# Norms on VectorE in the last half blocks, a residual by identity products, and unread products before the last turns

## The chip, the cores and the metric

The kernel runs on one core of one Trainium2 chip. A core has a matrix engine (TensorE, PE in the profile; its weight loads are PEld), three engines for elementwise work (VectorE or DVE, ScalarE or ACT, GpSimd or POOL), and a queue that issues transfers (SyncE or SP). Each takes its own instructions in order; they wait for each other by semaphores. The metric is the time of one execution on the device in microseconds (us), lower is better.

## The reference

One graph attention layer, over 8 frames of 2048 nodes with 256 channels, inside an outer residual and norm. The adjacency mask is one for all frames. Cut to what matters:

```python
q, k, v = split(x @ w_qkv)                       # 8 heads of 32 channels
scores = einsum('fnhd,fmhd->fhnm', q, k) / sqrt(32)
attn = softmax(where(adj > 0, scores, -1e9))
t = einsum('fhnm,fmhd->fnhd', attn, v)
y = layernorm(x + t) * g1 + be1
f = relu(y @ w1 + b1) @ w2 + b2
z = layernorm(y + f) * g2 + be2
out = layernorm(x + z)                           # no gain, no offset
```

Each row of the output passes through three norms. The last sum, `x + z`, is called the third residual here.

## The kernel before, in words

**Items.** `fast_path` walks over *items* `(f, qc, g, mb)`: frame, block of 512 query rows, group of four heads, and block of 128 key rows, `mb` from 0 to 15. For each item PE makes scores with keys on the partitions (L276), DVE adds the mask on the way from PSUM to SBUF in two halves of 128x1024 (L279), ACT exponentiates 128x2048 in place (L283), PE multiplies by the values (L310). The softmax sums are made from the exponentiated tiles: POOL adds some of them (L339), accumulating transfers add others (L336), and PE reduces the four tiles that remain (L382, "denominators").

**Order.** Each engine's order is that of the program text. Scores run two items ahead of the values. All other work (the `fill` list) consists of generators that `advance` resumes once per item: `yield 1` lets one item go by, `yield BANK` asks for a PSUM bank, and PE work draws on a *credit* per item, so a generator without credit waits for the next item unless it is due. While the loop runs only one bank is free for this side work (`bank()`, with `state["side"]` set), so a new product in that bank has to wait until the old one has been read.

**Rows.** When a query block is finished, `outcome` turns the attention output back to rows on PE and divides (`divide`, L427), adds `x`, and starts `tail`: norm (`norm`: statistics on DVE at L348 and L349, the factors `rs` and `nb` on POOL at L353 to L357, the application on ACT at L360), the two feed-forward products (`feed_forward`, L575 to L601), a second norm, `g2` and `be2` on POOL (L441, L443), the residual `x`, a third norm, and the store (L449). Normally the residual comes by an accumulating transfer; for the last block but one (block 2 of the last frame) DVE adds `xb`, a copy of `x` loaded earlier, at L411.

**The last block.** Its second head group (`ENDING`) is cut differently: 16 items of two key blocks by 256 query rows, half 0 first and then half 1 (scores L264, masks L268, values L298, output copy L303, POOL additions L330). Each half's rows are finished by a generator `closing(h)`: denominators (L490, five tiles), their sum (L493), turned sums and reciprocal (L504), turned output and division (L522), plus `x` (L525), statistics (`half_stats`, L456 and L457, `rs` on POOL at L459 and L460), first norm (`half_norm`: `nb` on DVE at L465, application on ACT at L467), POOL's row copy with `g1` and `be1 + b2` (L531, L532), turned rows and their scaling on ACT (L537), w1 (L545 copies it out), w2, the sum (L555), second norm, `g2` and `xb` on DVE (L560, L561), third norm, store (L565). Counts of the sums for a final range check (L508, L509, L971 to L982) go along.

After the loop `advance` is called until the list is empty. PE products through the helper `columns` have line L54, turns through `transposes` line L95.

Of the kernel before, what the change touches and what calls it, by code (L numbers as in the profile page):

```python
# [10 lines left out]
F32 = mybir.dt.float32  # L11
# [4 lines left out]
AF = mybir.ActivationFunctionType  # L16
ALU = mybir.AluOpType
AX = mybir.AxisListType

P = 128  # L20
# [41 lines left out]
def fast_path(ctx, tc, cst, x, adj, out, RS):  # L62
    nc = tc.nc
# [24 lines left out]
    def columns(out, lhsT, rhs, start, stop):  # L88
        state["credit"] -= 4 * out.shape[-1]
        in_columns(nc, out, lhsT, rhs, start, stop)  # L90
# [310 lines left out]
    def outcome(f, qc):  # L401
        yield ROOM
        state["tails"] += 1
        xin = x[f, qc * CH:(qc + 1) * CH, :].rearrange("(p j) c -> p j c", p=P)
        y = yp.tile([P, TPC, C], F32, name="y")
        begin = items.index((f, qc, 1, LAST)) + SUM + 2
        yield from divide(f, qc, y)
        if (f, qc) == (F - 1, NCK - 2):
            yield 1
            xb = state["xb"]  # L410
            nc.vector.tensor_tensor(y, y, xb, ALU.add)  # L411
            start(begin + 3, tail(f, qc, y, xin, 2, xb), begin + 18)
            return
        nc.gpsimd.dma_start(y, xin, accum_op=ALU.add)
        if (f, qc) == (F - 1, NCK - 3):
            start(begin + 10, tail(f, qc, y, xin, 2), begin + 18)
        else:
            start(begin + 10, tail(f, qc, y, xin), begin + 26)
# [12 lines left out]
    def tail(f, qc, y, xin, per=1, xb=None):  # L431
        yield from norm(y, per)
        yield from feed_forward(y)
        if xb is not None:
            nc.gpsimd.tensor_tensor(xb, xb, rows(cst["be2r"]), ALU.add)
        yield 1
        z = y
        yield from norm(z, per if per == 1 else TPC)
        while xb is None and per > 1 and state["now"] % MB not in CALM:
            yield 1  # L440
        nc.gpsimd.tensor_tensor(z, z, rows(cst["g2r"]), ALU.mult)  # L441
        yield 1
        nc.gpsimd.tensor_tensor(z, z, rows(cst["be2r"]) if xb is None else xb, ALU.add)  # L443
        yield 1
        if xb is None:
            nc.gpsimd.dma_start(z, xin, accum_op=ALU.add)
            yield 7 if per == 1 else 10
        yield from norm(z, per)
        nc.sync.dma_start(out[f, qc * CH:(qc + 1) * CH, :].rearrange("(p j) c -> p j c", p=P), z)  # L449
        state["tails"] -= 1  # L450

    def half_stats(t):
        mv = small.tile([P, 2, nc.vector.BN_AGGR_DIM], F32, name="mv")
        for j in range(2):
            st = small.tile([P, nc.vector.BN_STATS_DIM], F32, name="st")
            nc.vector.bn_stats(st, t[:, j, :])  # L456
            nc.vector.bn_aggr(mv[:, j, :], st)  # L457
        rs = small.tile([P, 2], F32, name="rs")
        nc.gpsimd.tensor_scalar(rs, mv[:, :, 1], EPS, 1.0, op0=ALU.add, op1=ALU.mult)  # L459
        nc.gpsimd.tensor_tensor(rs, rs, cst["mhalf"][:, 0:2], ALU.pow)  # L460
        return mv, rs

    def half_norm(t, mv, rs):
        nb = small.tile([P, 2], F32, name="nb")
        nc.vector.scalar_tensor_tensor(nb, mv[:, :, 0], -1.0, rs, op0=ALU.mult, op1=ALU.mult)  # L465
        for j in range(2):
            nc.scalar.activation(t[:, j, :], t[:, j, :], AF.Identity, bias=nb[:, j:j + 1], scale=rs[:, j:j + 1])  # L467

    def closing(h):
        f, qc, g = ENDING  # L470
        own, part, t0 = slice(2 * h, 2 * h + 2), slice(h * HQ, (h + 1) * HQ), len(items) - MB // 2 * (2 - h)
        terms = [(5, 6), (1, 7), (0, 7), (6, 8), (7, 8)]
        dst = out[f, qc * CH + h * HQ:qc * CH + (h + 1) * HQ, :].rearrange("(p j) c -> p j c", p=P)

        def row2(v):
            return v[:, None, :].to_broadcast([P, 2, C])

        yield BANK
        ps = bank()
        for n, (block, when) in enumerate(terms):  # L480
            if n:
                yield MORE
            while state["now"] < t0 + when:
                yield WAIT
            term = PT.pop((*ENDING, block + h * MB // 2))
            state["credit"] -= 4 * CH
            for b in range(2):
                for i in range(4):
                    r = D * i
                    nc.tensor.matmul(ps[r:r + D, 0:HQ], cst["halves"][:, g, :], term[:, i, b * HQ:(b + 1) * HQ],  # L490
                                     start=(n + b == 0), stop=(n + b == len(terms)))
        dT = DT[f, qc]
        nc.vector.tensor_tensor(dT[:, part], ps[:, 0:HQ], dT[:, part], ALU.add)  # L493
        if h == 0:
            state["y"] = yp.tile([P, TPC, C], F32, name="y")
            state["ff"] = [work.tile([P, 2, CH], F32, name=n) for n in ("turned", "hT")]
        y, (yT, hT) = state["y"][:, own], state["ff"]
        xr, xb = (t[:, own] for t in state["rows"])
        def turned_sums():
            ps = bank()  # L500
            transposes(ps, [dT[:, part][:, j::2] for j in range(2)])
            den = ps[:, 0:HQ].rearrange("p (j c) -> p j c", c=P)[:, :, ::D // 2]
            rc = op.tile([P, 2, H], F32, name="rc")
            nc.vector.reciprocal(rc, den)  # L504
            return rc, den

        def count(den):
            nc.vector.tensor_tensor(RS[:, 0, own], RS[:, 0, own], den, ALU.add)  # L508
            nc.vector.tensor_tensor(RS[:, 1, own], RS[:, 1, own], den, ALU.min)  # L509

        yield 1
        if h == 0:
            yield BANK
            rc, den = turned_sums()
            count(den)
        yield BANK
        po = bank()
        transposes(po, [OT[f, qc, gg][:, part][:, j::2] for gg in range(2) for j in range(2)])
        if h:
            rc, den = turned_sums()  # L520
        for gg in range(2):
            nc.vector.tensor_tensor(y[:, :, gg * P:(gg + 1) * P].rearrange("p j (h d) -> p j h d", d=D),  # L522
                                    po[:, gg * HQ:(gg + 1) * HQ].rearrange("p (j h d) -> p j h d", h=4, d=D),
                                    rc[:, :, gg::2, None].to_broadcast([P, 2, 4, D]), ALU.mult)
        nc.vector.tensor_tensor(y, y, xr, ALU.add)  # L525
        found = half_stats(y)
        if h:
            count(den)
        yield 1
        half_norm(y, *found)  # L530
        nc.gpsimd.tensor_tensor(xr, y, row2(cst["g1r"]), ALU.mult)  # L531
        nc.gpsimd.tensor_tensor(xr, xr, row2(cst["be1b2r"]), ALU.add)  # L532
        yield BANK
        ps = bank()
        transposes(ps, [y[:, j, a * P:(a + 1) * P] for a in range(2) for j in range(2)])
        for a in range(2):
            nc.scalar.activation(yT[:, a, part], ps[:, a * HQ:(a + 1) * HQ], AF.Identity,  # L537
                                 bias=cst["be1c"][:, a:a + 1], scale=cst["g1c"][:, a:a + 1])
        yield 1
        for d in range(2):  # L540
            yield BANK
            ps = bank()
            for a in range(2):
                columns(ps[:, 0:HQ], w1s[:, a, d * P:(d + 1) * P], yT[:, a, part], start=(a == 0), stop=(a == 1))
            nc.scalar.activation(hT[:, d, part], ps[:, 0:HQ], AF.Relu, bias=cst["b1s"][:, d:d + 1], scale=1.0)  # L545
        yield 1
        yield BANK
        ps = bank()
        for j in range(2):
            if j:  # L550
                yield MORE
            for d in range(2):
                columns(ps[:, j * C:(j + 1) * C], hT[:, d, part][:, j * P:(j + 1) * P], w2s[:, d, :], start=(d == 0), stop=(d == 1))
        z = y
        nc.vector.tensor_tensor(z, ps.rearrange("p (b c) -> p b c", c=C), xr, ALU.add)  # L555
        found = half_stats(z)
        yield 1
        half_norm(z, *found)
        yield 1
        nc.vector.tensor_tensor(z, z, row2(cst["g2r"]), ALU.mult)  # L560
        nc.vector.tensor_tensor(z, z, xb, ALU.add)  # L561
        found = half_stats(z)
        yield 1
        half_norm(z, *found)
        nc.sync.dma_start(dst, z)  # L565

# [39 lines left out]
    def start(t, gen, due):  # L606
        fill.append([t, gen, 1, due])
        fill.sort(key=lambda e: e[3])
# [408 lines left out]
```

## Time and profile before

| what | value |
|---|---|
| median of 3 executions | 3167.66 us (3167.57 to 3168.4) |
| the profiled execution | 3165.28 us, its span 3163.5 us |
| PE busy | 3071.6 us (97%) |
| DVE busy | 2751.4 us (87%) |
| ACT busy | 2423.8 us (77%) |
| POOL busy | 2589.8 us (82%) |
| PE busy, 3000 to 3050 us | 42.13 us of 50 |
| PE busy, 3120 to 3140 us | 10.78 us of 20 |
| last ACT instruction ends | 3159.32 us |

Times in the profile count from the start of the span. The shares are means over the whole program. A line of the timeline has the start in us, the busy time in us, engine, source line, operation, out<-in and the number of instructions merged into it; in brackets the engine's idle time before it and whose work ended it. PE counts fp32 products twice, as two passes, so four products appear as x8. A line of the windows view has the stretch, its length, the busy us of PE, PEld, DVE, ACT and POOL (with counts), then the granted clock of PE (1.00 is full), the share of the DMA engines and GB/s.

### The profile page before, as it was taken

How to read it: one execution, taken by the hardware profiler on the slowest of the kernel's cores; microseconds unless marked ns; L12 is line 12 of the kernel's file. 1: busy time of each engine (PE TensorE's matmuls, PEld its weight loads, DVE VectorE, ACT ScalarE, POOL GpSimd, SP SyncE). 2: the span in 40 equal slices, each digit the busy share in tenths (PEclk: the TensorE clock that was granted, in tenths of full speed). 3: DMA queues.
4: the chain of work that ended last, by engine and by line, in shares of the span. 5: the costliest groups of instructions: out<-in, count | busy, mean ns of one | idle time of the engine just before them, and what ended most of it. 6: DMA issues, size and time to landing. Idle time of an engine off the chain costs nothing.

```text
span 3163.5 us, 68998 instructions
## 1 busy us (share of the span) xinstructions
PE 3071.6 (97%) x29220; PEld 969.5 (31%) x29220; DVE 2751.4 (87%) x3138; ACT 2423.8 (77%) x1934; POOL 2589.8 (82%) x1358
## 2 busy tenths in 40 slices
PE   8899999999999999999999999999999999999986
PEld 4222233222332233322333323323233323332223
DVE  4989888998888998888988898888888888889885
ACT  4777777777778877778877878777778777778774
POOL 1768888888888988888888888888889888889885
PEclk9999999999999999999999999999999999999998
DMA  8998888988888988789878888879879888888861
GB/s 255 224 213 187 189 184 182 205 189 192 178 176 202 198 186 182 167 197 218 186 168 187 191 199 192 180 174 204 193 172 205 178 192 193 177 174 167 174 149 42
DMA packets 165467, 586.89 MB, mean 186 GB/s; under 512 B 15360, under 2 KB 84480, under 8 KB 116512
## 3 DMA queue, kind: packets, MB, share of 16 engines
q0 software_dynamic: 63696, 430.60, 69.0%
q1 hardware_dynamic: 100640, 150.50, 14.1%
q8 instruction: 231, 3.78, 0.5%
q10 hardware_dynamic: 816, 1.31, 0.1%
q14 instruction: 84, 0.69, 0.1%
HBM read 146.15 MB, written 37.75 MB: 58 GB/s over the span
## 4 chain that ended last, share of the span: by engine, by line


## 5 line engine op out<-in xcount | busy, mean ns | idle before, releaser
L279 DVE TENSOR_TENSOR p<-s,mask 128x1024 f32<-128x1024 f32 x2016 | 2371.1, 1218 | 302.3 <-PE s L276 170.2
L283 ACT ACTIVATE p<-p 128x2048 f32<-128x2048 f32 x1024 | 1955.8, 1910 | 565.3 <-DVE p L279 458.2
L339 POOL TENSOR_TENSOR p<-p 128x2048 f32<-128x2048 f32 x378 | 1845.1, 4881 | 332.7 <-ACT p L283 332.2
L276 PE MATMUL s<-qT,kT 32*128 32x512 f32 x8064 | 1152.4, 640 | 48.1 <-DVE p L279 44.7
L310 PE MATMUL x<-p,v 128*32 128x512 f32 x8064 | 1075.3, 605 | 3.0 <-ACT oT L314 3.0
L276 PEld LDWEIGHTS s<-qT,kT 32*128 32x128 f32 x8064 | 315.5, 183 | 653.6 <-DVE p L279 627.7
L336 POOL DMA_DIRECT2D p<-p x378 | 406.5, 1076 | 69.7 <-ACT p L283 49.4
L310 PEld LDWEIGHTS x<-p,v 128*32 128x32 f32 x8064 | 158.7, 108 | 768.2 <-issue 303.5
L382 PE MATMUL x<-p,halves 128*32 128x512 f32 x2016 | 261.1, 592 | 0.3 <-ACT turned L575 0.3
L54 PE MATMUL x<-in,wqkv 128*32 128x512 f32 x1888 | 245.6, 592 | 1.5 <-DVE y L170 0.8
L360 ACT ACTIVATE y<-y,nb,rs 128x256 f32<-128x256 f32 x372 | 218.3, 591 | 1.5 <-POOL nb L357 1.4
L348 DVE BATCH_NORM_STATS2 st<-y 128x6 f32<-128x256 f32 x372 | 154.7, 416 | 0.0
L54 PE MATMUL x<-turned,w1s 128*32 128x512 f32 (+1 forms) x1024 | 127.1, 593 | 0.0
L54 PEld LDWEIGHTS x<-wqkv,in 128*32 128x32 f32 x3584 | 102.2, 110 | 62.9 <-issue 54.5
L54 PE MATMUL x<-w2s,hT 128*32 128x256 f32 x2016 | 120.3, 379 | 0.0
L54 PE MATMUL x<-wqkv,in 128*32 128x128 f32 x3584 | 117.1, 273 | 0.0
L382 PEld LDWEIGHTS x<-p,halves 128*32 128x32 f32 x2016 | 65.4, 110 | 149.8 <-issue 147.2
L54 PEld LDWEIGHTS x<-in,wqkv 128*32 128x32 f32 x1888 | 61.1, 110 | 143.4 <-issue 115.1
L354 POOL TENSOR_TENSOR rs<-rs,mhalf 128x4 f32<-128x4 f32 x93 | 96.2, 1035 | 7.7
L441 POOL TENSOR_TENSOR y<-y,g2r 128x1024 f32<-128x1024 f32 x31 | 100.4, 3240 | 0.0
L443 POOL TENSOR_TENSOR y<-y,be2r 128x1024 f32<-128x1024 f32 x30 | 92.1, 3071 | 0.6
L54 PEld LDWEIGHTS x<-w2s,hT 128*32 128x32 f32 x2016 | 65.4, 110 | 68.9 <-issue 35.3
(155 smaller groups left out, 1423.1 us busy)
## 6 DMA issues: line engine op xcount, KB each, us to landing
p<-p POOLq DMA_DIRECT2D x380, 1024.0 KB, 10.1
in<-xd SPq DMA_DIRECT2D x87, 512.0 KB, 8.7
mask<-md SPq DMA_DIRECT2D x248, 128.0 KB, 8.5
y<-in_x_dram POOLq DMA_DIRECT2D x60, 512.0 KB, 9.7
out_dram<-y SPq DMA_DIRECT2D x31, 512.0 KB, 5.9
in<-in_x_dram SPq DMA_DIRECT2D x30, 512.0 KB, 10.3
xd<-in SPq DMA_DIRECT2D x28, 512.0 KB, 8.3
p<-in_adj_dram SPq DMA_DIRECT2D x8, 1024.0 KB, 14.1
```

Source lines behind the costliest of these rows:

```text
L54: nc.tensor.matmul(out[r:r + D], lhsT[:, r:r + D], rhs, start=start, stop=stop)
L276: nc.tensor.matmul(ps2[half][:, j, :], KT[f, mb // TPC, g][r:r + D, (mb % TPC) * P:(mb % TPC + 1) * P], QT[f, qc, g][r:r + D, :], start=Tr ...
L279: nc.vector.tensor_tensor(pt[:, 2 * half:2 * half + 2, :], ps, MK[f, qc, mb // 2][:, mb % 2, None, :].to_broadcast([P, 2, CH]), ALU.add)
L283: nc.scalar.activation(PT[item], PT[item], AF.Exp, scale=1.0 / math.sqrt(D))
L310: nc.tensor.matmul(O[grp][r:r + D, :], V[f, mb // TPC, g][:, mb % TPC, r:r + D], PT[item][:, h, :], start=(mb == 0), stop=(mb == LAST))
L336: nc.gpsimd.dma_start(PT[f, qc, g, chain[0]], PT.pop(item), accum_op=ALU.add)
L339: nc.gpsimd.tensor_tensor(first, first, PT.pop(item), ALU.add)
L348: nc.vector.bn_stats(st, t[:, j, :])
L354: nc.gpsimd.tensor_tensor(rs, rs, cst["mhalf"], ALU.pow)
L360: nc.scalar.activation(t[:, j, :], t[:, j, :], AF.Identity, bias=nb[:, j:j + 1], scale=rs[:, j:j + 1])
L382: nc.tensor.matmul(ps[r:r + D, :], cst["halves"][:, g, :], term[:, h, :], start=(n == 0), stop=(n == len(blocks) - 1))
L441: nc.gpsimd.tensor_tensor(z, z, rows(cst["g2r"]), ALU.mult)
```

## The change

Three things change, all in the work on the last frame. In `outcome`, for block 2, the third residual comes from products of the identity matrix with `xb`: two sets of four products into a PSUM bank, each followed by a DVE addition of half the rows. The tail starts at `begin + 4` in place of `begin + 3`, and without two pauses in `tail`. In the closing of the last block both halves' first and third norms are applied by DVE with one `tensor_scalar` per 256 columns; the second norm is folded into two `scalar_tensor_tensor` per 256 columns, `(z - mean) * g2` and `* rs + xb`, in place of `nb`, ACT's application and two DVE row operations. In half 1's closing five sets of four identity products write a bank that nothing reads, between the turned sums and the turned rows.

```diff
         yield from divide(f, qc, y)
         if (f, qc) == (F - 1, NCK - 2):
-            yield 1
             xb = state["xb"]
-            nc.vector.tensor_tensor(y, y, xb, ALU.add)
-            start(begin + 3, tail(f, qc, y, xin, 2, xb), begin + 18)
+            for j in range(0, TPC, 2):
+                yield BANK
+                ps = bank()
+                columns(ps, ident, xb[:, j:j + 2, :].rearrange("p j c -> p (j c)"), start=True, stop=True)
+                nc.vector.tensor_tensor(y[:, j:j + 2, :], ps.rearrange("p (j c) -> p j c", c=C), y[:, j:j + 2, :], ALU.add)
+            start(begin + 4, tail(f, qc, y, xin, 2, xb), begin + 18)
             return
...
         nc.gpsimd.tensor_tensor(z, z, rows(cst["g2r"]), ALU.mult)
-        yield 1
+        if xb is None:
+            yield 1
         nc.gpsimd.tensor_tensor(z, z, rows(cst["be2r"]) if xb is None else xb, ALU.add)
-        yield 1
         if xb is None:
+            yield 1
             nc.gpsimd.dma_start(z, xin, accum_op=ALU.add)
...
     def half_norm(t, mv, rs):
-        nb = small.tile([P, 2], F32, name="nb")
-        nc.vector.scalar_tensor_tensor(nb, mv[:, :, 0], -1.0, rs, op0=ALU.mult, op1=ALU.mult)
         for j in range(2):
-            nc.scalar.activation(t[:, j, :], t[:, j, :], AF.Identity, bias=nb[:, j:j + 1], scale=rs[:, j:j + 1])
+            nc.vector.tensor_scalar(t[:, j, :], t[:, j, :], mv[:, j, 0:1], rs[:, j:j + 1], op0=ALU.subtract, op1=ALU.mult)
...
         if h:
             rc, den = turned_sums()
+            again = bank()
+            for n in range(5):
+                columns(again, ident, OT[f, qc, 0], start=True, stop=True)
...
-        found = half_stats(z)
-        yield 1
-        half_norm(z, *found)
-        yield 1
-        nc.vector.tensor_tensor(z, z, row2(cst["g2r"]), ALU.mult)
-        nc.vector.tensor_tensor(z, z, xb, ALU.add)
+        mv, rs = half_stats(z)
+        for j in range(2):
+            nc.vector.scalar_tensor_tensor(z[:, j, :], z[:, j, :], mv[:, j, 0:1], cst["g2r"], op0=ALU.subtract, op1=ALU.mult)
+        yield 1
+        for j in range(2):
+            nc.vector.scalar_tensor_tensor(z[:, j, :], z[:, j, :], rs[:, j:j + 1], xb[:, j, :], op0=ALU.mult, op1=ALU.add)
         found = half_stats(z)
         yield 1
         half_norm(z, *found)
```

In the new program L411's addition is L414, the norm of the half blocks L469, the sum after w2 L560, the two folded operations L563 and L566, and the half blocks' denominators L492. Because the side work draws on the same credit, the order of PE's, ACT's and POOL's queues changes from the identity products on: the turned rows of the block before, its feed-forward products and the denominators stand one item later than in the old order; on ACT block 2's first norm pair follows an exponential that it used to precede, and its second norm stands ahead of the last exponential rather than ahead of the one before; in the closing half 0's turns now precede half 1's. Everything up to the first identity product is the same.

## Prediction

> **What bounds the kernel now.** I read the busy shares first, then the timeline of the last 160 us, then the granted clock in 1 us windows; the chain view is empty for this run. The page gives PE 97%, but the diff acts only after 3043 us, where the limit changes four times.
>
> ```profile
> 3044.71 4.52 POOL L339 TENSOR_TENSOR p<-p 128x2048 f32<-128x2048 f32 x1 [0.28 <-ACT p L283]
> 3045.31 5.01 DVE L411 TENSOR_TENSOR y<-y,in 128x1024 f32<-128x1024 f32 x1
> 3050.24 2.34 DVE L279 TENSOR_TENSOR p<-s,mask 128x1024 f32<-128x1024 f32 x2
> 3051.51 2.09 PE L276 MATMUL s<-qT,kT 32*128 32x512 f32 x8 [5.06 <-DVE p L279]
> ...
> 3074.99 0.76 ACT L575 ACTIVATE turned<-x,be1c,g1c 128x512 f32<-128x512 f32 x1
> 3075.81 1.06 PE L382 MATMUL x<-p,halves 128*32 128x512 f32 x8 [0.34 <-ACT turned L575]
> ```
>
> The residual addition L411 begins while POOL adds, and ends 1.09 us after POOL does (3049.23): it stood for about 4 us. Behind it the masks L279 stand, and so PE's scores. At 3075 ACT's queue is the limit: the denominator product L382 waits for the bank that the second "turned" copy frees.
>
> ```profile
> 3115.67 1.15 PE L264 MATMUL s<-qT,kT 32*128 32x256 f32 x16
> 3119.42 1.91 ACT L283 ACTIVATE p<-p 128x2048 f32<-128x2048 f32 x1 [0.35 <-DVE p L268]
> 3120.01 2.77 PE L490 MATMUL x<-p,halves 128*32 128x256 f32 x48
> 3123.46 1.91 PE L490 MATMUL x<-p,halves 128*32 128x256 f32 x32
> 3127.91 0.23 DVE L504 RECIPROCAL rc<-x 128x16 f32<-128x16 f32 x1
> 3133.93 0.13 DVE L465 SCALAR_TENSOR_TENSOR nb<-mv,rs 128x2 f32<-128x2 f32 x1
> 3134.09 1.09 ACT L467 ACTIVATE y<-y,nb,rs 128x256 f32<-128x256 f32 x2 [10.01 <-DVE nb L465]
> 3134.74 1.40 PE L95 MATMUL s<-ident,y 128*128 128x128 f32 x4 [7.60 <-ACT y L467]
> 3139.06 3.64 PE L54 MATMUL x<-turned,w1s 128*32 128x256 f32 x32
> 3146.69 0.69 DVE L555 TENSOR_TENSOR y<-s,in 128x512 f32<-128x512 f32 x1 [11.43 <-PE s L54]
> 3158.23 1.09 ACT L467 ACTIVATE y<-y,nb,rs 128x256 f32<-128x256 f32 x2 [0.19 <-DVE nb L465]
> ```
>
> After the last scores (3115.67) the path is PE's values and denominators, DVE from 3127.91, ACT's norms, PE at a poor clock, then DVE and ACT in turn to 3159.32; the store ends the span 4.2 us later.
>
> ```profile
> 3128.00:3129.00 1.00, 0.00 (x0) 0.00 (x0) 0.93 (x4) 0.00 (x0) 0.00 (x0) 1.00 0.00 0
> 3130.00:3131.00 1.00, 0.00 (x0) 0.00 (x0) 0.93 (x7) 0.00 (x0) 0.05 (x1) 0.50 0.00 0
> 3142.00:3143.00 1.00, 1.00 (x16) 0.49 (x12) 0.00 (x0) 0.23 (x1) 0.15 (x1) 0.50 0.00 0
> 3144.00:3145.00 1.00, 1.00 (x24) 0.57 (x20) 0.00 (x0) 0.61 (x2) 0.00 (x0) 1.00 0.00 0
> ```
>
> The column after the five engines is the clock: half after PE's idleness from 3127, whole again after 3143. Two w1 products (x32) took 3.4 us there, a w2 set (x32) at full clock 1.73 us.
>
> **What the Trainium skill says.** "SBUF — State Buffer", section "Who interferes with whom": a VectorE instruction with two SBUF inputs, or in a 2-port mode, and a GpSimd instruction lock each other out. L411 agrees. "VectorE: DVE Perf Modes", section "Mode 2×_2P": fp32 tensor_scalar in SBUF runs two elements per cycle, tensor_tensor one. L696 (128x1024, 0.686 us) against L279 (1.218) agrees. "TensorE: Matmul & The Clock Gate", Part 1: the clock follows PE's activity in free-running windows of 3.41 us. The trace agrees: half clock at 3013.6-3017.0, 3051.1-3054.6 and 3129.7-3143.3, each after a window with PE mostly idle, and all on one 3.41 us grid.
>
> **The change part by part.**
>
> *Third residual.* L411 goes. Two sets of four identity products come; a set like L382 costs PE 0.87 us in a stream. Two DVE additions of 128x512 with one operand in PSUM (like L427, 0.68) come, free of POOL's lock. Starts on DVE, from the spacings of before (masks 2.26, addition 0.60, two statistics 1.08): masks at 3043.05, addition 3045.31, masks 3045.91, addition 3048.17, masks 3048.77, statistics, masks 3052.11. PE fits between. The ending's first scores would start at 3063.45 instead of 3068.00.
>
> But 4.5 us doesn't survive. The identity products use up the planner's credit, `begin + 4` starts the tail one item later, and so all row work up to the fourth denominator product moves one item back in PE's and ACT's queues; on ACT an exponential that followed the first norm pair now precedes it. From that one's start at 3061.3 ACT has four exponentials (1.91 each), four norm pairs (1.08), oT (0.57) and two turned copies (0.76) to do before L382's first product, 14.05 us, with 0.4 idle: 3075.75, exactly where it was. Only the item count at that point differs: one more is behind. One item with one extra product is 2.94. Gain 2.9; the last scores start at 3112.7. Bounds 2 to 4.5.
>
> *End of the loop.* The fourth and fifth denominators of half 0 now follow the last scores, and all five of half 1 (x80) the last values. The last exponential waits behind the four norm steps of block 2, which in the old order stood before the exponential ahead of it. From the last scores T: values 1.07, product 0.89, values, product to T+4.6; PE idles until the exponential ends (T+4.66+1.91, so T+6.7); values 0.87, five denominators 4.33, end T+11.9. Before it was T+9.6. On DVE block 2's four statistics, which stood in the path (3125.78 to 3128), now lie under these products: POOL's two row operations end at T+9.6, the statistics at T+11.9. The first reciprocal comes at R = T+12.5, before T+12.25. Loss 0.3. If the 2.1 us idleness brings half clock for one window, 1.7 more.
>
> *Norms by VectorE.* R to the end of the second half's statistics was 6.1 us and stays so (sum of the same rows). Then two L469 per half, each (128+147)/0.96 = 0.29 us (estimate from L696's rate), in place of nb 0.13, a hand-over and 1.09 on ACT. First half done at R+6.7, turned on PE to R+7.4, ACT copies to R+8.5. POOL's rs for the second half comes at R+7.1; norm to R+7.8, turned to R+8.65, copied to R+9.7 (before R+12.3). w1 begins at R+8.7 behind the turns in PE's queue: four products of 0.87, then w2 1.73 and 0.2 latency: the sum L560 starts at R+14.1 at full clock (before R+18.78). Bound above: when POOL's row multiply takes the port ahead of the second norm, 1.27, or twice that.
>
> *Unread products.* Five sets of 0.87 = 4.4 us, from R+0.5 to R+4.9. The rows are needed at R+6.7, so they hide under DVE's work. At half clock they take 8.7, end at R+9.2, and delay the turns by 2.5. They shorten PE's idleness, yet 3.8 us remain from R+4.9 to R+8.7, broken by two turns of 0.65. I take one window at half clock near w1: +1.4 (bounds 0 and 1.7). L560 then starts at R+15.5: gain 3.3.
>
> *After L560.* Before, 12.63 us (3146.69 to 3159.32). Now on DVE, with 0.41 per scalar_tensor_tensor (a 128x256 row, L522 0.418): sums 0.73 twice, statistics four times 1.1 with 0.2 of small flags, eight such instructions 3.3, then POOL's rs 1.1 and the last norm 0.58: 11.1, and 0.2 because the first half's norm holds the port against that rs. Gain 1.3 (bounds 0.6 and 1.8: before, L459 and L460 grew by 0.8 together beside DVE's two-input additions at 3154).
>
> *Without cost.* Block 2's last norm on ACT now lies between the hT copies of the halves: 1.05 us, while PE has half 1's w1 and half 0's w2 to do; uncovered, it would cost 1.05. Its store precedes the last ones on SP's queue as before. The sum counts (L508, L509) move behind the second half's statistics: 0.23, inside the 6.1. The identity products wait for a load long landed. The dropped pauses of the tail change nothing in POOL's order.
>
> Sum against the profiled span 3163.5: -2.9 +0.3 -3.3 -1.3 = -7.2, span 3156.3. That execution took 3165.28; the median of the runs shown, 3167.66, lies 2.4 above it. Less the same 7.2 it is 3160.5.
>
> **The rivals.**
> - *Fully warm and no collision*: no half-clock window. For: unread products fill R+0.5 to R+4.9. Against: 3010.3 to 3012.5, idle for 2.3 us, was enough for half clock. 7.2+1.4 = 8.6: 3159.1.
> - *The port lock moves*: POOL's two row operations (L531 and L532 of before, 1.27 each) get ahead of the second norm's two instructions. Both wait for the same rs, so it is a race: 7.2-2.5 = 4.7, 3163.0.
> - *The clock stays down, slower than before*: the new idleness at T+4.6 leaves half clock and it doesn't come back before the end. Half 1's denominators +4.3, turns +2.5 behind the unread products and +0.75 themselves, w1 +3.45, w2 +1.75: 12.8 against the warm 8.6, so 4.2 slower: 3171.9. It decides from about 8.6 us of such loss. Against: full windows at 3051 to 3054 and 3140 to 3143 brought the clock back.
> - *The change doesn't do what it says*: were L411's 5 us a wait for its load, the identity product would wait too. Its load was issued some 40 us earlier and landing takes 10.3; little chance, counted in the second case.
>
> **How the numbers follow.** Chances: forecast 0.58, warm 0.18, lock 0.17, clock down 0.07. About 0.2% (6.3 us) is what a measurement can tell. Within the forecast six parts in seven lie beyond it: 0.50, with warm 0.18 and 0.02 of the lock 0.70 faster; the rest of both and 0.02 of the last case 0.25 within; 0.05 slower. The range 3157.6 to 3163.8 takes in warm with the loop's upper bound and most of the lock case.
>
> **What would show it.** No DVE instruction of 5 us and no PE gap over 3 us near 3045; the ending's first scores near 3063.5, the last near 3112.7; an idle PE of 2 us ahead of the last values; unread products of about 4.4 us that end before the second half's statistics; the first norm on DVE near 0.3 us each; ACT without L467. I am wrong if the ACT queue gives the loop's gain back wholly, if unread products run at half clock, or if one of DVE's new two-input instructions lasts over 1 us.

## The result and the profile after

The changed kernel takes 3162.68 us (median of 18 executions, 3158.53 to 3164.7), the kernel before beside it 3167.91 us (18 executions, 3165.78 to 3170.08). The ratio is 0.9982 with a 95% interval of 0.9975 to 0.9988: 5.7 us less by the ratio, 3.8 to 7.9 by its interval. The forecast was 3160.5 and 7.2 less. Of all executions of this document one was far off, of the kernel e9 below: 7373.85 us, at a mean granted clock of 0.407; it is left out of that kernel's ratio but not of its median, no trace of it was kept, and its cause is open.

The two profiled spans differ by less than that (3163.5 and 3160.3), for a reason that has nothing to do with the change. Block 2's second division on DVE (L427 before, L430 now) is the last mark ahead of the first new instruction. It starts at 3042.45 in the old trace and at 3046.13 in the new one, with the same instructions ahead of it on every engine. In all thirteen traces of this document these are the same, and the division starts anywhere from 3042.27 to 3048.86; two traces of the changed kernel have it at 3046.13 and 3044.85. One visible difference is the clock: in the new trace PE is at half clock from 21.8 to 25.2 us and for one window from 158.3 us on, where the old trace has full clock; in return it misses one of before at 3013. How much of the 3.68 us these windows make was not tried. So I count every trace from that division on, and from there the change gains 6.88 us:

| stretch | before | changed | difference |
|---|---|---|---|
| division to the last scores | 73.22 | 69.44 | -3.78 |
| last scores to the last reciprocal | 15.24 | 15.34 | +0.10 |
| last reciprocal to the sum after w2 (L555, L560) | 15.78 | 14.91 | -0.87 |
| that sum to the end of the last compute instruction | 12.63 | 10.91 | -1.72 |
| from there to the end of the span | 4.18 | 3.57 | -0.61 |
| sum | 121.05 | 114.17 | -6.88 |

(Spans are given to 0.1 us, so the last stretch and the sum are good to 0.05. The forecast counts the closing from the first of the two reciprocals, R, which stands 3.0 to 3.1 us ahead of the last.) The timeline of the changed kernel, with start, duration, engine, line, operation and, in brackets, the idle time before and its releaser:

```profile
3048.40 4.58 POOL L339 TENSOR_TENSOR p<-p 128x2048 f32<-128x2048 f32 x1 [0.29 <-ACT p L283]
...
3048.99 0.68 DVE L414 TENSOR_TENSOR y<-x,y 128x512 f32<-128x512 f32 x1
...
3067.17 1.15 PE L264 MATMUL s<-qT,kT 32*128 32x256 f32 x16 [1.19 <-DVE p L279]
...
3115.57 1.15 PE L264 MATMUL s<-qT,kT 32*128 32x256 f32 x16
...
3121.97 1.07 PE L298 MATMUL x<-p,v 128*32 128x256 f32 x16 [1.66 <-ACT p L283]
...
3127.83 0.26 DVE L506 RECIPROCAL rc<-x 128x16 f32<-128x16 f32 x1
...
3128.92 4.50 PE L54 MATMUL s<-oT,ident 128*32 128x512 f32 x40
...
3132.15 0.56 POOL L353 TENSOR_SCALAR rs<-mv 128x4 f32<-128x4 f32 x1
...
3133.91 0.73 DVE L469 TENSOR_SCALAR y<-y,mv,rs 128x256 f32<-128x256 f32 x2
...
3134.17 0.21 POOL L357 TENSOR_SCALAR nb<-nb 128x4 f32<-128x4 f32 x1
...
3134.78 0.71 POOL L464 TENSOR_TENSOR rs<-rs,mhalf 128x2 f32<-128x2 f32 x1
...
3135.46 1.26 POOL L536 TENSOR_TENSOR in<-y,g1r 128x512 f32<-128x512 f32 x1
3135.52 2.69 DVE L469 TENSOR_SCALAR y<-y,mv,rs 128x256 f32<-128x256 f32 x2 [0.87 <-POOL rs L464]
...
3136.80 1.26 POOL L537 TENSOR_TENSOR in<-in,be1b2r 128x512 f32<-128x512 f32 x1
...
3139.10 3.99 PE L54 MATMUL s<-turned,w1s 128*32 128x256 f32 x48
...
3145.82 0.69 DVE L560 TENSOR_TENSOR y<-x,in 128x512 f32<-128x512 f32 x1 [7.24 <-PE x L54]
...
3155.99 0.74 DVE L469 TENSOR_SCALAR y<-y,mv,rs 128x256 f32<-128x256 f32 x2 [0.59 <-POOL rs L464]
```

Read it from the top. POOL adds from 3048.40 on as before, but DVE's addition beside it takes 0.68 us in place of 5.01: one of its two operands comes from PSUM. The ending's first scores come 21.04 us after the division, before 25.56. PE still idles 1.66 us ahead of the last values, behind ACT. Then look at the two pairs of L469 in the first norm. The first pair takes 0.73 us. The second takes 2.69: POOL's row operation L536 began 0.06 us ahead of it, and L537 followed. I call this the lock, as in the prediction: a DVE and a POOL instruction that don't run side by side. ACT is out of this path, and the norm is still late. (e4 and e2 below test that the lock is the reason.)

The granted clock of the changed kernel in four stretches of one window each (columns: stretch, length, busy us of PE, PEld, DVE, ACT, POOL with counts, then PE's clock):

```profile
3131.34:3134.75 3.41, 2.36 (x22) 0.58 (x14) 3.17 (x11) 0.00 (x0) 2.92 (x6) 1.00 0.00 0
3134.75:3138.16 3.41, 0.80 (x5) 0.40 (x4) 2.64 (x3) 1.02 (x2) 3.20 (x3) 1.00 0.00 0
3138.16:3141.57 3.41, 3.31 (x27) 1.70 (x31) 0.42 (x5) 1.49 (x3) 2.54 (x2) 0.50 0.00 0
3141.57:3144.98 3.41, 3.41 (x68) 1.92 (x64) 0.00 (x0) 2.68 (x8) 0.00 (x0) 1.00 0.02 5
```

While DVE stands in the lock, PE has 0.80 us of work in the second stretch, and the third, in which w1 starts, runs at half clock.

### The profile page after: what moved, and what is told of

Read it like the earlier page. It is cut to its first block, busy times and chain, and to the rows that moved or that the text cites. A ratio compares the mean times of both kernels' runs of the same rounds, so it can differ in the third digit from the quotient of the medians.

```text
span 3160.3 us, 69095 instructions
## 1 busy us (share of the span) xinstructions
PE 3076.0 (97%) x29276; PEld 970.1 (31%) x29276; DVE 2753.2 (87%) x3145; ACT 2417.0 (76%) x1922; POOL 2589.8 (82%) x1358
## 3 DMA queue, kind: packets, MB, share of 16 engines
q8 instruction: 231, 3.78, 0.5%
## 4 chain that ended last, share of the span: by engine, by line
PE 77%; DVE 9%; issue 2%; DMA 1%; POOL 1%; ACT 1%; DVEq 0%; POOLq 0%; ACTq 0%
PE s L276 28%; PE x L310 25%; PE x L54 15%; DVE p L279 7%; PE x L382 6%; PE x L95 3%; DMA p<-p 1%; DVE st L348 1%; DVE dT L388 1%; POOL p L339 0%; PE s L264 0%; DVE y L430 0%; ACT p L283 0%; PE x L298 0%; DVE p L268 0%
## 5 line engine op out<-in xcount | busy, mean ns | idle before, releaser
L382 PE MATMUL x<-p,halves 128*32 128x512 f32 x2016 | 261.6, 593 | 0.7 <-ACT turned L580 0.6
L382 PEld LDWEIGHTS x<-p,halves 128*32 128x32 f32 x2016 | 65.4, 110 | 151.1 <-issue 147.3
```

What stands on the lines that cost most here:

```text
L382: nc.tensor.matmul(ps[r:r + D, :], cst["halves"][:, g, :], term[:, h, :], start=(n == 0), stop=(n == len(blocks) - 1))
```

## The experiments

The theory after this reading was: (a) the third residual by identity products gains 3.8 us up to the last scores and nothing is given back there; (b) the norms on DVE lose about 2 us to POOL's row operations; (c) the unread products are worth little, since the clock falls anyway. The rivals were that the order at the end of the loop takes (a) back, that half clock and not the lock limits the norms, and that the unread products are needed. All times of one line of this table come from that kernel's own profile; the medians stand beside those of the kernel before, run on the same chip.

| kernel | median, before beside it | ratio, 95% interval | division to last scores | to last reciprocal | to sum after w2 | to last compute | to end | sum |
|---|---|---|---|---|---|---|---|---|
| before | | | 73.22 | 15.24 | 15.78 | 12.63 | 4.18 | 121.05 |
| changed | 3162.68, 3167.91 | 0.9982 (0.9975-0.9988) | 69.44 | 15.34 | 14.91 | 10.91 | 3.57 | 114.17 |
| e1 residual alone | 3165.65, 3169.26 | 0.9993 (0.9985-1.0001) | 69.46 | 15.34 | 16.08 | 12.63 | 4.46 | 117.97 |
| e2 norms alone | 3163.66, 3169.26 | 0.9982 (0.9975-0.9988) | 73.24 | 15.27 | 12.11 | 10.90 | 3.79 | 115.31 |
| e3 no unread | 3163.78, 3169.26 | 0.9981 (0.9975-0.9988) | 69.47 | 15.35 | 15.02 | 10.91 | 3.59 | 114.34 |
| e4 joined rows | 3160.17, 3169.26 | 0.9971 (0.9960-0.9983) | 69.47 | 15.35 | 13.04 | 10.90 | 3.66 | 112.42 |
| e5 joined, no unread | 3160.22, 3169.20 | 0.9972 (0.9962-0.9982) | 69.45 | 15.34 | 13.33 | 10.90 | 3.61 | 112.63 |
| e6 joined, six unread | 3160.32, 3169.20 | 0.9970 (0.9958-0.9983) | 69.45 | 15.35 | 11.40 | 10.89 | 3.68 | 110.77 |
| e7 block 2 later | 3158.39, 3169.20 | 0.9965 (0.9952-0.9979) | 69.45 | 14.67 | 10.84 | 10.91 | 5.13 | 111.00 |
| e8 and its store earlier | 3157.47, 3168.35 | 0.9963 (0.9949-0.9976) | 69.44 | 14.68 | 10.82 | 10.89 | 3.68 | 109.51 |
| e9 e8 with six unread | 3157.40, 3168.35 | 0.9967 (0.9954-0.9980) | 69.44 | 14.66 | 10.83 | 10.90 | 3.66 | 109.49 |
| e10 e8 with no unread | 3160.65, 3169.43 | 0.9969 (0.9957-0.9981) | 69.45 | 14.67 | 12.99 | 10.90 | 3.66 | 111.67 |
| e11 changed, again | 3163.40, 3169.43 | 0.9981 (0.9971-0.9990) | 69.45 | 15.33 | 14.99 | 10.90 | 3.68 | 114.35 |

Of the first four stretches, those with the same code and the same clock repeat within 0.03 us from trace to trace. That is why differences of a few tenths can be read here, which the medians can't tell. The clock is the exception. Its windows of 3.41 us form a grid that lies differently over every trace: the division stands 0.13 to 3.32 us behind an edge of it. Where a stretch is at half clock in one profile, another execution of the same kernel can have full clock. For such stretches I therefore also slide a stretch of 3.41 us along the trace and look how little work of PE it can hold; from all traces together, a window with less than 1.55 us was always followed by half clock, one with more than 1.65 never (last section).

### e1: the residual alone

The first two hunks of the diff, in the kernel before; the second, which drops two pauses of the tail, is not repeated:

```diff
-            nc.vector.tensor_tensor(y, y, xb, ALU.add)
-            start(begin + 3, tail(f, qc, y, xin, 2, xb), begin + 18)
+            for j in range(0, TPC, 2):
+                yield BANK
+                ps = bank()
+                columns(ps, ident, xb[:, j:j + 2, :].rearrange("p j c -> p (j c)"), start=True, stop=True)
+                nc.vector.tensor_tensor(y[:, j:j + 2, :], ps.rearrange("p (j c) -> p j c", c=C), y[:, j:j + 2, :], ALU.add)
+            start(begin + 4, tail(f, qc, y, xin, 2, xb), begin + 18)
```

> The kernel before with the third residual by identity products (and the tail's new start and pauses) alone; the closing's norms stay on ACT and there are no unread products. Theory: the 5 us stall of L411 is what this part removes, and about 3.8 us of it lives to the last scores: from the first scores of the differing part to the last scores about 70.4 us (before 74.13), last scores to first reciprocal about 12.3, and the closing as in the kernel before (first reciprocal to the sum after w2 about 18.8, from there to the last compute instruction about 12.6). Whole time 3.5 to 4 us less than before. Rival: the new order at the end of the loop gives it back (last scores to first reciprocal 14 us or more): 0 to 2 us less.

To the last scores 69.46 (70.38 from the first scores of that part), and from there to the first reciprocal 12.25. The whole gain of the loop is here and the order at its end costs nothing: the first rival falls. The closing is 0.3 us longer and the store's part 0.28, so 3.08 remain, a little under what was expected. The executions alone don't show a gain clear of zero (the ratio reaches 1.0001). The timeline of e1 has the lock already:

```profile
3132.91 1.26 POOL L535 TENSOR_TENSOR in<-y,g1r 128x512 f32<-128x512 f32 x1
3132.97 1.22 DVE L469 SCALAR_TENSOR_TENSOR nb<-mv,rs 128x2 f32<-128x2 f32 x1 [1.36 <-POOL rs L464]
```

The second half's `nb` on DVE takes 1.22 us here, and 0.16 in the kernel before. So it is this part of the change that puts POOL's row operation right behind the second `rs`.

### e2: the norms alone

The hunks of the half blocks' norms and of the folded second norm, in the kernel before; the first of them:

```diff
-            nc.scalar.activation(t[:, j, :], t[:, j, :], AF.Identity, bias=nb[:, j:j + 1], scale=rs[:, j:j + 1])
+            nc.vector.tensor_scalar(t[:, j, :], t[:, j, :], mv[:, j, 0:1], rs[:, j:j + 1], op0=ALU.subtract, op1=ALU.mult)
```

> The kernel before with the half blocks' norms applied by VectorE alone; the third residual stays an addition on DVE and there are no unread products. Theory: the loop is as before (74.1 us from the first scores of that part to the last), the second norm of the first kind meets POOL's two row operations (about 2.7 us for its two instructions instead of 0.73), so the sum after w2 starts 0 to 1 us earlier against the first reciprocal than before (18.8), and what follows is 1.7 us shorter, the store's part 0.6: 2.3 to 3.3 us less than before in all. Rival: the lock is avoided by chance here and the gain is 4 us or more; other rival: without the unread products the clock is lower for longer and takes it back, under 1.5 us.

It gains 5.74 us, and 3.67 of it where the changed kernel gains 0.87. My expectation was wrong: the lock isn't met, as its first rival said, though not by chance. The timeline of e2 shows why:

```profile
3137.94 0.74 POOL L460 TENSOR_TENSOR rs<-rs,mhalf 128x2 f32<-128x2 f32 x1
3138.71 0.74 DVE L465 TENSOR_SCALAR y<-y,mv,rs 128x256 f32<-128x256 f32 x2 [0.59 <-POOL rs L460]
3138.76 0.20 POOL L353 TENSOR_SCALAR rs<-mv 128x4 f32<-128x4 f32 x1
3139.04 1.01 POOL L354 TENSOR_TENSOR rs<-rs,mhalf 128x4 f32<-128x4 f32 x1
...
3140.57 1.27 POOL L529 TENSOR_TENSOR in<-y,g1r 128x512 f32<-128x512 f32 x1
```

Between the factor `rs` that releases the second norm (L460) and the row operations (L529) POOL has block 2's factors to make, L353 to L357. When L529 starts, the norm has been done for 1.12 us. In the changed kernel these four stand ahead of this `rs` (3132.15 to 3134.38), as block 2's tail comes earlier in the closing; the row operation, that of the first half, is then POOL's very next instruction. Whether the tail's new start or its dropped pauses moved them was not tried. So the two parts of the change work against each other: e1 and e2 together gain 3.08 + 5.74 = 8.82, the changed kernel 6.88, e3 (both parts, no unread products) 6.71. These are profiles; the ratios of e2 and of the changed kernel are the same.

### e3: no unread products

```diff
-            again = bank()
-            for n in range(5):
-                columns(again, ident, OT[f, qc, 0], start=True, stop=True)
```

> The changed kernel without the five sets of unread products. Theory (the unread products shorten the half clock around w1 to one window): first reciprocal to the sum after w2 1.5 to 3 us longer than in the changed kernel (17.99), PE at half clock for two windows or more after the first reciprocal; the whole 1.5 to 3 us longer. Rival (a window at half clock comes either way, so they do nothing): 0 to 0.5 us of difference, one window at half clock in both.

The rival holds for the time: 0.17 us more in the profile, and a ratio of 0.9981 beside 0.9982. It doesn't hold for the clock, which is half for three windows here, from 3134.3 to 3144.6, and for one in the changed kernel. What decides, as I read it, is when the clock comes back relative to w1. That is 2.7 us after w1's start here and 2.5 in the changed kernel, and the second norm, late by the lock, lasts 2.69 us in both. That the changed kernel loses a window is no accident of its grid: stretches of a window's length with under 1.55 us of work start anywhere from 3132.66 to 3136.09, a range as long as a window.

### e4: POOL's rows behind the second norm

```diff
-        nc.gpsimd.tensor_tensor(xr, y, row2(cst["g1r"]), ALU.mult)
-        nc.gpsimd.tensor_tensor(xr, xr, row2(cst["be1b2r"]), ALU.add)
+        if h:
+            both = state["rows"][0]
+            nc.gpsimd.tensor_tensor(both, state["y"], rows(cst["g1r"]), ALU.mult)
+            nc.gpsimd.tensor_tensor(both, both, rows(cst["be1b2r"]), ALU.add)
```

> The changed kernel with POOL's two row operations of the halves (row copy times g1, plus be1 + b2) made once for both halves, behind the second half's norm, so that they can't take the port ahead of it. Theory (the lock of POOL's row operations costs the second norm 2.0 us): the second half's two norm instructions take about 0.73 us instead of 2.69, the sum after w2 starts 1.5 to 2 us earlier against the first reciprocal than in the changed kernel (17.99), the whole 1.5 to 2 us less. Rival (PE is left at half clock for one window anyway, so that w1 and w2 are stretched by what was won): 0 to 0.7 us less.

1.87 us less between the last reciprocal and the sum after w2, 1.75 in all: the lock's price, as the theory had it. The timeline of e4:

```profile
3133.67 0.71 POOL L464 TENSOR_TENSOR rs<-rs,mhalf 128x2 f32<-128x2 f32 x1
...
3134.41 0.74 DVE L469 TENSOR_SCALAR y<-y,mv,rs 128x256 f32<-128x256 f32 x2 [0.88 <-POOL rs L464]
...
3135.23 2.36 POOL L538 TENSOR_TENSOR in<-y,g1r 128x1024 f32<-128x1024 f32 x1 [0.85 <-DVE y L469]
```

POOL now waits for the norm (0.85 us idle), and DVE takes 0.74. The clock still falls for one window. The same four stretches of one window, for e4:

```profile
3128.57:3131.98 3.41, 3.41 (x36) 0.91 (x28) 3.21 (x10) 0.00 (x0) 1.75 (x4) 1.00 0.00 0
3131.98:3135.39 3.41, 1.53 (x11) 0.77 (x8) 2.46 (x14) 1.02 (x2) 2.23 (x6) 1.00 0.00 0
3135.39:3138.80 3.41, 3.41 (x31) 1.56 (x34) 0.13 (x2) 1.50 (x3) 3.33 (x2) 0.50 0.02 5
3138.80:3142.21 3.41, 3.41 (x68) 1.92 (x64) 0.00 (x0) 2.89 (x7) 1.23 (x1) 1.00 0.00 0
```

1.53 us of work in 3.41 were too little to keep the clock; the full stretch after it brought it back.

### e5 and e6: none and six of the unread sets, with the lock gone

e5 drops the sets from e4, with the edit of e3:

> The kernel of e4 (POOL's row operations joined behind the second norm) without the five unread sets. Theory (the unread products only move the time of the half clock, since about 1.6 us of work in the window before w1 is too little): last reciprocal to the sum after w2 12.1 to 13.3 us (e4 13.04, e2 without unread products 12.11), the whole within 0.7 us of e4. Rival (they are worth something once the collision is gone): last reciprocal to that sum 14.5 us or more, the whole 1.5 us or more longer than e4.

e6 adds one to e4:

```diff
-            for n in range(5):
+            for n in range(6):
```

> The kernel of e4 with six unread sets in place of five. Theory (how much PE does in the one window before w1 decides; 0.9 us more lifts it from about 1.6 to 2.5 us of 3.41): no half clock between the first reciprocal and the sum after w2, last reciprocal to that sum 11.6 us or less (e4 13.04), the whole about 1.4 us less than e4. Rival (the idleness that remains falls into one window in any case, as the windows' start is by chance): 0 to 0.5 us of difference in the median, half clock for one window as in e4.

e5 is 0.29 us longer than e4 from the last reciprocal to the sum after w2, and its median is the same. e6 has full clock from the last scores to that sum and gains 1.64 us in its profile (13.04 to 11.40), as the theory said; its median of 6 executions, 3160.32, shows none of it against 3160.17.

The sliding stretch tells why both comparisons depend on luck. In e4 it holds under 1.55 us of work only where it starts from 3131.54 to 3132.33, and under 1.65 from 3131.44 to 3132.43; the grid of e4's profile has an edge at 3131.98, right there. These are 0.79 to 0.99 us of 3.41, so about a quarter of the possible grids cost e4 a window (an estimate from where PE's work lies in this one trace). In e6 every such stretch holds 1.75 us or more, and no grid costs a window. In e5 it is empty at worst, and every grid does: the starts with too little span 5.63 us. So in most executions e4 should run like e6, and the five sets should be worth more there than the 0.29 us. No run shows that: the medians' intervals (0.9958 to 0.9983 for e6) are wider than what is asked.

### e7 and e8: block 2's last norms out of the way

e7, against e4:

```diff
-    def norm(t, per=1):
+    def norm(t, per=1, pause=2):
...
-        yield 2
+        yield pause
...
-        yield from norm(z, per if per == 1 else TPC)
+        yield from norm(z, per if per == 1 else TPC, 2 if xb is None else 3)
...
-        yield from norm(z, per)
+        if xb is not None:
+            yield 3
+        yield from norm(z, TPC if xb is not None else per, 2 if xb is None else 1)
```

> The kernel of e4 with block 2's second norm one item later, so that on ACT it stands behind the last exponential, and its third norm's four statistics behind the second half's first norm on DVE. Theory (PE's 1.66 us of idleness ahead of the last values are ACT's four norm steps ahead of the last exponential, and nothing else takes their place): last scores to last reciprocal 13.5 us instead of 15.35, the idleness under 0.2 us, closing from the last reciprocal as in e4 within 0.3, the whole about 1.8 us less than e4. Rival (the copy of the output on ACT, now behind the norm steps, or POOL's rows meeting the addition of x on DVE take it back): 0 to 0.8 us less.

Half of this was wrong. PE's idleness ahead of the last values falls to 0.98 us, not under 0.2, and the stretch to 14.67, not 13.5. The timeline of e7:

```profile
3119.51 1.91 ACT L283 ACTIVATE p<-p 128x2048 f32<-128x2048 f32 x1 [1.18 <-DVE p L268]
...
3121.32 2.06 ACT L360 ACTIVATE y<-y,nb,rs 128x256 f32<-128x256 f32 x4
3121.47 1.07 PE L298 MATMUL x<-p,v 128*32 128x256 f32 x16 [0.98 <-ACT p L283]
...
3134.47 0.74 DVE L471 TENSOR_SCALAR y<-y,mv,rs 128x256 f32<-128x256 f32 x2 [0.32 <-POOL rs L466]
...
3150.87 0.34 SPq L574 DMA_DIRECT2D out_dram<-y  x1
3151.33 0.85 SPq L455 DMA_DIRECT2D out_dram<-y  x1
3152.27 0.38 SPq L574 DMA_DIRECT2D out_dram<-y  x1
```

With ACT's norm steps gone from in front of it, the last exponential waits 1.18 us for its mask on DVE: the next wait in line. Unforeseen was the other gain, 2.20 us after the last reciprocal. Block 2's factors are out of POOL's queue there, so the second norm waits 0.32 us for its own in place of 0.88. The rest, 1.64, is what e6 gained as well, the window at half clock of e4's profile: e7 has none, and its emptiest stretch holds 2.09 us. And block 2's store (L455) now falls between the stores of the halves: 5.13 us from the last compute to the end, in place of 3.66.

e8, against e7:

```diff
-        yield from norm(z, TPC if xb is not None else per, 2 if xb is None else 1)
+        yield from norm(z, TPC + 1 if xb is not None else per, 2 if xb is None else 1)
```

> The kernel of e7 with one pause less inside block 2's third norm, so that its factors on POOL stand ahead of the half blocks' second norms, and its store ahead of theirs. Theory (in e7 the store of block 2 fell between the halves' stores and lengthened the end by 1.5 us): last compute instruction to end of span about 3.6 us instead of 5.13, the rest as in e7, the whole about 1.5 us less than e7. Rival (the end is as long because POOL's factors of block 2, or ACT's norm of it, now delay the halves): sum after w2 to the last compute instruction over 11.5 us, no gain.

It came out so: 3.68 at the end, the rest unchanged. 11.54 us less than before from the division on. It has the lowest ratio of the kernels, 0.9963 (0.9949 to 0.9976), at 3157.47 us.

### e9 and e10: six and none of the unread sets in e8

The same two edits as in e6 and e5.

> The kernel of e8 with six unread sets. Theory (in e8 the idleness ahead of w1 is about 1.5 us in all, which seldom fills enough of one window): within 0.4 us of e8. Rival (the sixth set still removes a half clock window in part of the runs): 0.5 to 1.4 us less than e8 in the median.

> The kernel of e8 without the five unread sets. Theory (unread products are worth something only where the idleness left beside them is short enough for the clock to stay full: in e8 they leave about 1.5 us): half clock from before w1 on, last reciprocal to the sum after w2 12 to 13.5 us (e8 10.82), the whole 1 to 2 us more than e8. Rival (they are worth nothing here either, as in e3 and e5): within 0.5 us of e8.

e9 is as e8, as expected. e10 is 2.16 us longer, all of it between the last reciprocal and the sum after w2, at half clock from 3132.9 to 3139.7. So the unread products do pay in e8, by what they were there for, and paid next to nothing in the changed kernel. This rests on the profiles: the ratios differ by 0.0006, some 1.9 us, with intervals that overlap. It isn't luck of the grid, as starts with too little work span 5.15 us in e10 and don't exist in e8. One line of the windows view of e8, with the same columns, the emptiest stretch of a window's length around w1's start:

```profile
3133.11:3136.52 3.41, 2.09 (x20) 1.31 (x24) 3.06 (x17) 1.52 (x4) 1.95 (x3) 1.00 0.00 0
```

2.09 us of work at worst, and the clock stays full. In e4, with five sets as well, the window ahead of the fall had 1.53 us.

### e11: the changed kernel again

> The changed kernel itself, once more, beside the kernel of e10 on one chip. Theory (the collision of the second norm with POOL's row operations is fixed by the order and not by chance): its two instructions take about 2.7 us again, last reciprocal to the sum after w2 14.9, the time about 5 us less than before. Rival (a race of 0.06 us falls either way from run to run): 0.7 us and 13 us.

Where the lock stands, the order decides, not chance. The timeline of e11:

```profile
3134.18 1.26 POOL L536 TENSOR_TENSOR in<-y,g1r 128x512 f32<-128x512 f32 x1
3134.24 2.69 DVE L469 TENSOR_SCALAR y<-y,mv,rs 128x256 f32<-128x256 f32 x2 [0.88 <-POOL rs L464]
```

POOL is ahead by 0.06 us, as in the changed kernel's first profile and in e3.

## Why the prediction came out as it did

The time lay inside the range, 2.2 us above the forecast, and 6.88 us on the comparable stretch against 7.2 forecast is close. That is luck: two errors of some 2 us cancelled, so the single steps say more.

*Third residual, the stall.* Forecast 4.55 us earlier at the ending's first scores, measured 25.56 - 21.04 = 4.52. No wait for the load showed up in place of the lock, so "the change doesn't do what it says" is out. (The load of `xb`, L746, was issued at 2989.20 in the old trace, 56 us ahead of L411 and not 40.)

*Third residual, what ACT leaves of it.* Forecast -2.9, measured -3.78 in the changed kernel and -3.76 in e1. The mechanism was right: L382's first product waited 0.58 us for the second turned copy, ACT's queue was the limit. The term that was mis-sized is "14.05 us, with 0.4 idle". It added durations, and ACT's rows overlap. The timeline of ACT in the changed kernel:

```profile
3073.43 1.09 ACT L360 ACTIVATE y<-y,nb,rs 128x256 f32<-128x256 f32 x2
3074.42 0.76 ACT L580 ACTIVATE turned<-x,be1c,g1c 128x512 f32<-128x512 f32 x1
3075.08 1.90 ACT L283 ACTIVATE p<-p 128x2048 f32<-128x2048 f32 x1
3076.88 1.08 ACT L360 ACTIVATE y<-y,nb,rs 128x256 f32<-128x256 f32 x2
3077.87 0.77 ACT L580 ACTIVATE turned<-x,be1c,g1c 128x512 f32<-128x512 f32 x1
```

Each starts 0.09 to 0.10 us before the one ahead of it ends (3073.43 + 1.09 = 3074.52 against 3074.42). Over the whole stretch, from 3065.08 to 3078.64, it was 13.56 us where the sum said 14.45. From start to start, not durations, is what such a queue has to be added from.

*End of the loop.* Forecast +0.3 at the first reciprocal, measured 12.26 against 12.25 us. PE idled 1.66 us there (2.1 forecast) without half clock.

*Norms by VectorE.* Forecast -3.3, measured -0.8 to -0.9. This is the step that failed. The prediction had the right collision among its rivals ("POOL's two row operations ... get ahead of the second norm's two instructions") and put its price at 2.5, where the pair measured 2.69 - 0.73 = 1.96 more, and e4 gained 1.87 without it. What was wrong was "Both wait for the same rs, so it is a race", and the chance of 0.17 that followed from it. The row operation is that of the first half, whose norm ended at 3134.65; it waits for nothing but its turn in POOL's queue. POOL makes the `rs` of the second half, and the row operation is its next instruction; the norm on DVE has to wait for the news of it. It came 0.06 us later in three of three profiles. The Trainium skill says it in so many words ("SBUF — State Buffer", section "Who interferes with whom"): "Issue order, not op shape, decides who blocks." The traces agree, with 2.69 us for one order and 0.73 for the other. The order was to be read from the queues: I wrote that "the dropped pauses of the tail change nothing in POOL's order". With the tail's new start and pauses the queue did change: block 2's four factor instructions, which kept the two apart in e2, moved ahead of `rs`. e2, with the old queue, gains 3.67, near the 3.3 forecast. A smaller slip is the price of the norm itself: it was taken from L696, which makes bf16 from int32 and is no fp32 instruction, as 0.29 us each; L469 took 0.41 each and 0.73 to 0.74 the pair where no lock was met.

*Unread products.* One window at half clock near w1 was forecast and came, from 3138.16 to 3141.57. That the products buy much in this kernel was not so: 0.17 us by e3. What they buy depends on what idleness is left beside them, and e10 shows 2.16 us once it is short. The rival "clock stays down" did not come about: from the last scores to the sum after w2 the clock fell at most once, and where it fell it was back before that sum, in every profile.

*After L560.* Forecast -1.3, measured -1.72, and e2 alone has it too. The next instruction starts 0.76 to 0.79 us after a new pair starts, where 0.82 was taken; POOL's `rs` beside them grew to 0.33 + 0.83 us and hid.

*The end.* -0.61 from the last compute instruction to the end of the span wasn't in the sum. By e1 (+0.28) and e2 (-0.39) it goes with the norms; what in the stores causes it was not tried.

Together: -3.78 + 0.01 - 0.79 - 1.72 - 0.61 = -6.89 counted from the first reciprocal. The loop, the rows after L560 and the end brought 2.2 us more than forecast, the norms 2.5 less.

## What to carry to other kernels

When an operation moves onto DVE, read the queue of POOL at that place: if the engine that releases the DVE instruction has as its own next instruction one that DVE's can't run beside, expect it to win (it did in all four profiles here that had this order), and a few small instructions between the two (e2), or the long ones put behind (e4), are worth the whole lock. Two parts of a change that don't touch each other in the text can meet in such a queue, so price the parts alone and together. Work given to PE to hold its clock paid here only where what was left idle in one window was short (e8), so count the idle time beside it first, and fill it last, when the waits around it are gone. And before one profile at half clock is compared with another at full clock, slide a window's length along the trace: it tells whether the code costs the window or only the grid of that execution.

## What the runs showed of the hardware

- The clock doesn't need an idle window to fall. "TensorE: Matmul & The Clock Gate", Part 1 of the Trainium skill, puts half clock after an idle window of about 3.4 us. Here a window with 1.53 us of work of 3.41 was enough (e4), with no idleness longer than 1.05 us in it.
- The thirteen traces together show where it turns. Laid on the grid of their own half-clock stretches, they have 11,873 windows at full clock. The 51 that were followed by half clock hold up to 1.65 us of PE's work, and the 11,822 others 1.55 us or more. So it turns between these two, a little under half of the window. PE's busy time is modelled, and this is a limit of that time. The windows of the two extremes, each with the one behind it, of e11 (kept) and e10 (fell):

```profile
17.33:20.74 3.41, 1.55 (x60) 1.28 (x48) 1.14 (x2) 1.05 (x2) 0.88 (x4) 1.00 1.04 376
20.74:24.15 3.41, 2.71 (x24) 1.40 (x28) 0.63 (x2) 1.07 (x2) 0.00 (x0) 1.00 1.07 380
...
54.04:57.45 3.41, 1.65 (x12) 0.63 (x16) 2.75 (x3) 0.31 (x1) 0.00 (x0) 1.00 0.23 77
57.45:60.86 3.41, 3.41 (x20) 0.59 (x16) 2.77 (x3) 1.91 (x1) 0.00 (x0) 0.50 0.00 0
```

- To come back takes more work than to stay. Of the 73 windows at half clock, the 35 that were followed by another hold up to 2.80 us of work (e3, from 21.37), and those followed by full clock 2.65 or more (changed kernel, from 158.32).
- The return takes one window with enough work, and it comes at the grid's next edge: after 3.41 us of work in e4 and 3.31 in the changed kernel. It is 2.5 us after w1's start in the changed kernel and 2.7 in e3, although e3's clock had been low for two windows longer.
- A DVE pair that meets two POOL operations of 1.26 us takes 2.69 us. In the changed kernel its first instruction ends at 3136.87 and its second at 3138.21, each 0.15 us after one of the two POOL operations.
